# Layer 1, first pass: centring by 64x64 products, norm factors spread by 32-row products, and the second strip loaded earlier

## The chip, the core and the metric

The kernel runs on one core of a Trainium2 chip, in float32 throughout. The metric is device microseconds of one execution. Three executions of the kernel before took 8789.25 to 8792.47 us, with a median of 8791.17 us.

The core's engines are named as the profile names them: PE (TensorE, matrix products and transposes), PEld (its weight loads), DVE (VectorE), ACT (ScalarE), POOL (GpSimd) and SP (SyncE, which issues all the transfers here). Each engine works through its own queue in order; they wait for each other through semaphores.

## The reference, cut to what matters

The input is a 4 x 64 x 256 x 256 image. Layer 0 (a gated convolution) gives an image of the same shape. Layer 1, where the change lies, is this:

```python
def _layer_norm(x, g, b):
    mu = jnp.mean(x, axis=-1, keepdims=True)
    var = jnp.mean((x - mu) ** 2, axis=-1, keepdims=True)
    return (x - mu) * jax.lax.rsqrt(var + EPS) * g + b

def _s5_block(x, i, ...):
    fx = _layer_norm(x, ln1_g[i], ln1_b[i])
    h = _s5_scan(fx, ...)              # a linear recurrence, forward and backward
    x = jax.nn.gelu(h) + fx
    fx2 = _layer_norm(x, ln2_g[i], ln2_b[i])
    return fx2 @ ff_enc[i].T @ ff_dec[i].T + fx2

v = _gn(x)                             # group norm, 32 groups over 64 channels
y_h = _s5_block(v, row by row, 0)      # pixels in row order
y_v = _s5_block(v, column by column, 1)
x = x + concat([y_h, y_v], channels) @ fusion_w.T + fusion_b
```

The first layer norm runs over the 64 channels of each pixel, and both directions share it up to the gain `g` and the bias `b`: the centred and scaled value `z = (x - mu) * rsqrt(var + EPS)` is the same.

## The kernel before

Layer 0 comes first and writes its result into DRAM (`x1d[b]`, one per image `b`). Then, for each of the four images, `pass_a` and `pass_b` run one after the other. `pass_a` normalises the image, stores the normalised values `fv` (for the column direction) and `fh` (for the row direction) in DRAM for `pass_b`, and computes a summary of each group of 16 pixels along both directions. The scan at the start of `pass_b` turns the summaries into states, and the rest of `pass_b` computes the outputs. Only `pass_a`, and the few lines that load its strips, are changed.

`pass_a` works on 16 strips of 16 rows. A strip is loaded by four transfers of 256 KB into a tile `[128, 8, 256]`; the tile's two halves of 64 partitions hold 64 channels each, so that a column of the tile is two pixels. The ring of strip tiles has two buffers, which `pass_b` uses too. A software pipeline runs over 20 turns: in turn `n` strip `n` is centred, strip `n-1` gets its variances, strip `n-2` is scaled and stored, strip `n-3` gets its mirrored sums and differences, and strip `n-4` its summaries. The steps are functions, and a loop at the end of `pass_a` calls them in a fixed order. The wrappers `vec`, `act`, `gps` and `mm` keep the program's order on DVE, ACT, POOL and PE, so this order of calls is the order of every queue.

The steps before, with the tile names under which the profile lists them:

- `centre(s, i)`, four times in a strip: one 128x128 product over 512 columns (`pc`) subtracts the channel mean of both halves and applies the group norm; ACT reads the product twice, to write the centred values `xc` and the squares `sq`, 512 columns each.
- `sums(s)`: four products with 32 output rows each gather the squares into `pv`, and ACT copies it to `sums`.
- `rstd_of(s)`: four transposes (`pv`) bring the variances to two columns in 32; DVE adds the epsilon (`ve`), and POOL takes the power -1/2 (`rs`), in one instruction of 5.43 us.
- `widen(s)`: ACT puts the 32 factors of each partition back into PSUM, and DVE copies them 64-fold into `rw`, `[128, 32, 64]`.
- `affine(s, i)`, four times: four transposes of `rw` (`pr`) give the factors of 512 columns for all partitions; DVE multiplies them with `xc` and writes `z`, with the pixels of a row reordered.
- `scaled_in(s, i)`, four times: ACT writes `fv` and `fh` from `z`, with gain and bias.
- `mirrored(s, d)`: sums and differences of `fv` (DVE) or `fh` (POOL) with themselves mirrored (`sd`).
- `summary_columns(s, k)` (`pt`) and `summary_rows(s, k)` (`ps`): the products of the summaries, two groups each; ACT copies one half of each result to `m`.
- `place_columns(s)` and `place_rows(s)`: DVE adds and subtracts the halves into the state arrays `sf` and `sb`.
- `store(s)`: SP writes `fv` and `fh` to DRAM. The strip loads stand in the same SP queue.

In the order of calls, `affine`, `scaled_in` and `centre` alternate with the other steps in quarters of a strip. The helper lines of the profile are L1102 (`mm`), L1106 (transposes), L164 (ACT and POOL), L303 (DVE); a group is told by its tile names.

[...]

Of the kernel before, what the change touches and what calls it, by code (L numbers as in the profile page):

```python
# [11 lines left out]
AF = mybir.ActivationFunctionType  # L12
# [24 lines left out]
def _layout(parts):  # L37
    at, n = {}, 0
    for name, width in parts:
# [3 lines left out]


CONST_AT, CONST_N = _layout(
    [("ident", 128), ("swap", 128), ("nswap", 128), ("cen", 128), ("gm", 128), ("on2", 34), ("sgn", 1), ("qf", 64),
     ("qi2", 128), ("qj", 128), ("selt", 128)]
)

# [9 lines left out]
def _constants():  # L59

    out = np.zeros((P, CONST_N), np.float64)

    def put(name, a):
        o, w = CONST_AT[name]
        out[: a.shape[0], o : o + w] = a

    eye = np.eye(P)
    swap = np.roll(eye, C, axis=0)
    put("ident", eye)
    put("swap", swap)  # L70
    put("nswap", -swap)
    put("cen", eye - np.kron(np.eye(2), np.full((C, C), 1.0 / C)))
    pair = np.kron(np.eye(C // 2), np.ones((2, 2)))
    put("gm", np.kron(np.ones((2, 2)), pair) / 4.0)
    put("on2", np.kron(np.eye(2, 34, 2), np.full((C, 1), 1.0 / C)))
    put("sgn", np.concatenate([-np.ones((C, 1)), np.ones((C, 1))]))

    r, c = np.meshgrid(np.arange(8), np.arange(8), indexing="ij")  # L80
    q, sel = [], []
    for k1 in range(8):
        for k2 in range(5):
            own = k1 in (0, 4) and k2 in (0, 4)
            if k2 in (0, 4) and k1 > 4:
                continue
            w = np.zeros(40)
            w[k1 * 5 + k2] += 0.5
            w[((8 - k1) % 8 if k2 in (0, 4) else k1) * 5 + k2] += 0.5
            ang = 2 * np.pi * (k1 * r + k2 * c) / 8  # L90
            q.append(np.cos(ang).ravel() / 8 * (1 if own else math.sqrt(2)))
            sel.append(w)
            if not own:
                q.append(np.sin(ang).ravel() / 8 * math.sqrt(2))
                sel.append(w)
    q, sel = np.array(q), np.array(sel)
    assert q.shape == (64, 64) and np.allclose(q @ q.T, np.eye(64))
    put("qf", np.concatenate([q.T, q.T]))
    qi2 = np.zeros((2, 64, 2, 4, 2, 8))
    for pc in range(2):  # L100
        qi2[pc, :, :, :, pc] = q.reshape(64, 4, 2, 8).transpose(0, 2, 1, 3)
    put("qj", qi2.reshape(128, 2, 4, 8, 2).transpose(0, 1, 4, 2, 3).reshape(128, 128))
    for pc in range(2):
        qi2[pc, :, :, :, pc] = q.reshape(64, 2, 4, 8)
    put("qi2", qi2.reshape(128, 128))
    put("selt", np.concatenate([sel, sel]).T)
    return out.astype(np.float32)
# [3 lines left out]
def tile_kernel(ctx: ExitStack, tc: tile.TileContext, x, cst, w0, winp, wdwp, w1, out):  # L111
# [14 lines left out]
    def con(name):  # L126
        o, w = CONST_AT[name]
        return ct[:, o : o + w] if o < CONST_0 else tables[0][:, o - CONST_0 : o - CONST_0 + w]

    ident, swap, nswap = con("ident"), con("swap"), con("nswap")  # L130
    mhalf = new(cpool, [P, 32], "mhalf")
    nc.vector.memset(mhalf, -0.5)

# [941 lines left out]
        return t  # L1075


    norms = new(gpool, [P, nb, 2], "norms", 1)
    with tc.tile_pool(name="psn", bufs=2, space=PSUM) as pn:
        for b in range(nb):  # L1080
# [8 lines left out]
    def pass_a(b, x0):  # L1089
        with ExitStack() as es:  # L1090
            wp = es.enter_context(tc.tile_pool(name="wa", bufs=1))
            wk = es.enter_context(tc.tile_pool(name="wka", bufs=2))
            pp = es.enter_context(tc.tile_pool(name="psa", bufs=2, space=PSUM))
            wa = [new(wp, [P, NA[d], P], f"wa{d}") for d in range(2)]
            for d in range(2):
                nc.sync.dma_start(out=wa[d].rearrange("p a b -> p (a b)"), in_=wda[d])
# [8 lines left out]
                for k in range(4):  # L1105
                    tc.keep_in_program_order(nc.tensor.transpose(ps[:, k * P : (k + 1) * P], v(k), ident))  # L1106

            def centre(g, i):
                ps = new(pp, [P, 512], "pc")
                mm(ps, lhsT=cen, rhs=g["x"][:, 2 * i : 2 * i + 2, :].rearrange("p a b -> p (a b)"), start=True, stop=True)  # L1110
                xc, sq = new(wk, [P, 512], "xc", 9), new(wk, [P, 512], "sq", 5)
                act.activation(xc, ps, AF.Identity, bias=off)
                act.activation(sq, ps, AF.Square, bias=off)
                g["xc", i], g["sq", i] = xc, sq

            def sums(g):

                ps = new(pp, [P, 512], "pv", 1)
                for i in range(4):
                    mm(ps[32 * i : 32 * i + 32], lhsT=con("on2")[:, 2:34], rhs=g.pop(("sq", i)), start=True, stop=True)  # L1120
                g["sums"] = new(wk, [P, 512], "sums", 1)
                act.copy(g["sums"], ps)

            def rstd_of(g):

                ps, v = new(pp, [P, 512], "pv", 1), g.pop("sums")
                turn_blocks(ps, lambda k: v[:, k * P : (k + 1) * P])
                ve, r = new(wk, [P, 16, 2], "ve"), new(wk, [P, 32], "rs")
                vec.tensor_scalar(ve, ps.rearrange("p (n c) -> p n c", c=32)[:, :, 0:2], LN_EPS, None, ALU.add)
                gps.tensor_tensor(r, ve.rearrange("p n c -> p (n c)"), mhalf, ALU.pow)  # L1130
                g["rs"], g["by"] = r, ps

            def widen(g):

                g["r"], ps = new(wk, [P, 32, C], "rw"), g.pop("by")
                act.copy(ps[:, :32], g.pop("rs"))
                vec.tensor_copy(g["r"], ps[:, :32].unsqueeze(2).to_broadcast([P, 32, C]))

            def affine(g, i):

                if i == 0:
                    g["fv"], g["fh"] = new(wk, [P, 8, 256], "fv"), new(wk, [P, 16, 128], "fh")
                ps, z = new(pp, [P, 512], "pr"), new(wk, [P, 2, 16, 16], "z")
                turn_blocks(ps, lambda k: g["r"][:, 8 * k + 2 * i : 8 * k + 2 * i + 2].rearrange("p a c -> p (a c)"))
                vec.tensor_tensor(
                    z.rearrange("p r q g -> p r g q"), g.pop(("xc", i)).rearrange("p (r g q) -> p r g q", r=2, q=16),
                    ps.rearrange("p (r g q) -> p r g q", r=2, q=16), ALU.mult,
                )
                g["z", i] = z

            def scaled_in(g, i):
                z = g.pop(("z", i))
                act.activation(
                    g["fv"][:, 2 * i : 2 * i + 2].rearrange("p r (q g) -> p r q g", q=16), z, AF.Identity,
                    bias=par(1, "b1"), scale=par(1, "g1"),
                )
                act.activation(
                    g["fh"].rearrange("p q (r g) -> p q r g", r=8)[:, :, 2 * i : 2 * i + 2], z.rearrange("p r q g -> p q r g"),
                    AF.Identity, bias=par(0, "b1"), scale=par(0, "g1"),
                )  # L1160

            def mirrored(g, d):

# [50 lines left out]

            got = {0: {"x": x0}}

            def at(s, step, *args):
                if 0 <= s < NS1:  # L1220
                    step(got[s], *args)

            for n in range(NS1 + 4):
                if n + 1 < NS1:
                    got[n + 1] = {"x": load_strip(b, n + 1)}
                at(n, centre, 0)
                at(n - 2, affine, 0)
                at(n - 1, sums)
                at(n - 2, scaled_in, 0)
                at(n - 3, mirrored, 1)  # L1230
                at(n - 4, summary_columns, n - 4, 1)
                at(n - 1, rstd_of)
                at(n, centre, 1)
                at(n - 2, affine, 1)
                at(n - 2, scaled_in, 1)
                at(n - 4, place_columns, n - 4)
                at(n - 4, summary_rows, n - 4, 0)
                at(n, centre, 2)
                at(n - 2, affine, 2)
                at(n - 1, widen)  # L1240
                at(n - 2, scaled_in, 2)
                at(n - 4, summary_rows, n - 4, 1)
                at(n, centre, 3)
                at(n - 2, affine, 3)
                at(n - 4, place_rows, n - 4)
                at(n - 2, scaled_in, 3)
                at(n - 2, store, n - 2)
                at(n - 3, summary_columns, n - 3, 0)
                at(n - 3, mirrored, 0)

    def scan(tabs):
        with ExitStack() as es:
# [5 lines left out]
                nc.sync.dma_start(out=rot[d], in_=rotd[d])  # L1258

            fold = new(wp, [P, 3, C], "fold")  # L1260
            nc.vector.tensor_tensor(fold[:, 0], ident[:, 0:C], swap[:, 0:C], ALU.add)
            nc.vector.tensor_tensor(fold[:, 1], ident[:, 0:C], nswap[:, 0:C], ALU.add)
            nc.vector.tensor_tensor(fold[:, 2], ident[:, C:P], nswap[:, C:P], ALU.add)
            turns = [tabs[:, 4 * d : 4 * d + 4].rearrange("p (k a) c -> p k (a c)", k=2) for d in range(2)]
# [49 lines left out]
    def pass_b(b):  # L1314

        with ExitStack() as es:
# [201 lines left out]
            for n in range(len(order) + 3):  # L1518
                if n < len(order):
# [4 lines left out]
                    if d == 0 and s + 1 < NS1:  # L1524
                        accs[s + 1] = load_strip(b, s + 1)
                    elif d == 0 and b + 1 < nb:
                        accs[NS1] = load_strip(b + 1, 0)
                for i in range(4):
                    m, group = (n, 3) if i == 0 else (n + 1, i - 1)

# [16 lines left out]
                    late(1)  # L1547
        return accs.get(NS1)

    first = load_strip(0, 0)  # L1550
    for b in range(nb):
        pass_a(b, first)
        first = pass_b(b)
# [77 lines left out]
```

## Time and profile before

| Stretch of the profiled execution | us |
|---|---|
| its own time, from the first instruction to the last | 8795.4 |
| layer 0 (0 to 4041) | 4041 |
| first `pass_a`, from the first centring to the last summary | 260.0 |
| the other three, from the same point to the same point | 268.4, 269.2, 268.2 |
| all four | 1065.8 |
| one turn of `pass_a` in its steady part | 14.63 |

The profile recorded this one execution; its own time is its span, and there is no other record of it. The span is 4.2 us (0.05%) above the median of the three timed executions. PE was granted a clock of 0.988 on average.

The turn is taken from the starts of the first centring product of each strip. In the first image they stand at 4101.02, 4115.66, 4130.29, 4144.92 us and so on: from the sixth strip to the last one they are 14.63 us apart, in all four images. The first five turns of the first image take 6.55, 6.99, 14.53, 15.11 and 16.73 us. From the start of the last strip's first centring to the end of the last summary it takes 53.75 us.

A line of a list of groups reads: source line, engine, operation, output tile and input tiles, shapes, count, then busy time in total, the mean of one in ns, and the idle time of the engine before the group with what ended it. A line of a timeline reads: start, length, engine, line, operation, tiles, shapes and count of a run of equal instructions. Each float32 product appears as two matmuls.

### The profile page before, as it was taken

What the parts mean: (1) busy time and instruction counts of PE and PEld (TensorE: products, weight loads), DVE (VectorE), ACT (ScalarE), POOL (GpSimd) and SP (SyncE); (2) the same over time, 40 slices, a digit from 0 to 9 for tenths busy, and PEclk for the clock granted to TensorE, in tenths of its full rate; (3) what the DMA queues carried; (4) which work ended last, traced back from release to release, by engine and by line L of the source; (5) the groups of instructions that cost most, each with busy time, mean ns of one, the idle gap of its engine ahead of it and who ended that gap; (6) DMA issues with size and microseconds to landing.
All of it is one profiled execution on the core that took longest, in us unless ns stands there. A gap on an engine that the chain in (4) does not pass through costs nothing. (4 is left out here: it accounts for less than half of the span.)

```text
span 8795.4 us, 184922 instructions
## 1 busy us (share of the span) xinstructions
PE 8386.9 (95%) x79478; PEld 5721.3 (65%) x79478; DVE 7055.1 (80%) x8837; ACT 3411.4 (39%) x5158; POOL 2401.9 (27%) x1282
## 2 busy tenths in 40 slices
PE   3999999999999999998999989999989999899999
PEld 2666666666666666665566657566655666565666
DVE  6999999999999999996767657776757677576766
ACT  3444444444444444445522237222264222462222
POOL 3000000000000000003734446544456444474444
PEclk9999999999999999999999999999999999999999
DMA  7444344444444333334423336133263233452332
GB/s 174 106 102 103 98 103 101 104 102 98 103 104 101 87 88 84 84 80 142 151 68 82 91 90 214 59 80 89 73 183 116 80 82 80 123 196 53 82 89 65
DMA packets 655264, 904.19 MB, mean 103 GB/s; under 512 B 43120, under 2 KB 584816, under 8 KB 618864
## 3 DMA queue, kind: packets, MB, share of 16 engines
q1 hardware_dynamic: 654448, 892.37, 37.9%
q8 instruction: 627, 10.27, 0.5%
q14 instruction: 189, 1.55, 0.1%
HBM read 583.86 MB, written 275.05 MB: 98 GB/s over the span
## 5 line engine op out<-in xcount | busy, mean ns | idle before, releaser
L207 PE MATMUL m<-v,sw 64*128 64x256 f32 (+1 forms) x8192 | 1542.8, 393 | 1.5 <-DVE v L303 1.1
L207 PEld LDWEIGHTS m<-v,sw 64*128 64x128 f32 (+1 forms) x8192 | 1123.4, 188 | 504.0 <-issue 359.0
L303 DVE SCALAR_TENSOR_TENSOR acc<-xat,taps,acc 128x1024 f32<-128x1024 f32 x1024 | 1311.0, 1280 | 16.6 <-ACT acc L164 2.9
L1446 POOL TENSOR_TENSOR xr<-xr,fx 128x512 f32<-128x512 f32 x512 | 650.3, 1270 | 1862.3 <-ACT xr L1445 1367.7
L1351 PE MATMUL pst<-fx,wb 64*128 64x256 f32 (+1 forms) x4992 | 1016.1, 438 | 37.5 <-DVE stm L303 18.3
L694 POOL MEMSET at<- 64x256 f32 x4 | 1.2, 308 | 3526.2 <-DVE v L303 3526.2
L1351 PEld LDWEIGHTS pst<-fx,wb 64*128 64x128 f32 (+1 forms) x4992 | 508.8, 187 | 370.4 <-issue 244.1
L1476 POOL TENSOR_TENSOR rs<-ve,mhalf 128x32 f32<-128x32 f32 x128 | 695.3, 5432 | 99.5 <-DVE ve L303 99.5
L303 DVE SCALAR_TENSOR_TENSOR stm<-stm,step,pst 128x512 f32<-128x512 f32 x640 | 478.5, 748 | 232.9 <-PE pst L1351 219.4
L1447 ACT ACTIVATE sq<-xr 128x512 f32<-128x512 f32 x512 | 322.9, 631 | 873.7 <-POOL xr L1446 873.7
L207 PEld LDWEIGHTS m<-ct,hw 128*64 128x64 f32 x16384 | 509.8, 138 | 117.6 <-issue 117.6
L303 DVE SCALAR_TENSOR_TENSOR sto<-sto,step,pst 128x512 f32<-128x512 f32 x512 | 382.9, 748 | 242.4 <-PE pst L1351 231.1
L1351 PE MATMUL px<-wb,xr 128*128 128x128 f32 x4096 | 574.1, 284 | 0.0
L1351 PEld LDWEIGHTS px<-wb,xr 128*128 128x128 f32 x4096 | 524.2, 194 | 54.0 <-issue 41.8
L303 DVE TENSOR_TENSOR y<-px,rs 128x512 f32<-128x512 f32 x512 | 354.0, 691 | 230.6 <-PE px L1351 221.6
L1351 PE MATMUL ph<-sto,wb 128*64 128x128 f32 (+1 forms) x5120 | 528.1, 299 | 0.0
L207 PE MATMUL m<-ct,hw 128*64 128x64 f32 x16384 | 527.4, 223 | 0.0
L1351 PE MATMUL ph<-stm,wb 128*64 128x128 f32 (+1 forms) x5120 | 525.1, 299 | 0.0
L1351 PEld LDWEIGHTS ph<-stm,wb 128*64 128x64 f32 (+1 forms) x5120 | 409.3, 147 | 144.2 <-issue 127.9
L1351 PEld LDWEIGHTS ph<-sto,wb 128*64 128x64 f32 (+1 forms) x5120 | 405.3, 147 | 142.7 <-issue 129.6
L1445 ACT ACTIVATE xr<-ph 128x512 f32<-128x512 f32 x256 | 152.8, 597 | 825.9 <-PE ph L1351 825.9
L164 POOL TENSOR_TENSOR rs<-ve,mhalf 128x32 f32<-128x32 f32 x64 | 347.6, 5432 | 398.5 <-DVE ve L303 386.8
(317 smaller groups left out, 15636.0 us busy)
## 6 DMA issues: line engine op xcount, KB each, us to landing
strip<-x1d SPq DMA_DIRECT2D x512, 256.0 KB, 7.3
fx<-fxd SPq DMA_DIRECT2D x128, 1024.0 KB, 6.9
at<-in_x_dram SPq DMA_DIRECT2D x248, 320.0 KB, 4.6
sx<-in_x_dram SPq DMA_DIRECT2D x256, 256.0 KB, 4.0
pr<-in_x_dram SPq DMA_DIRECT2D x256, 256.0 KB, 4.1
er<-in_x_dram SPq DMA_DIRECT2D x256, 256.0 KB, 4.0
x1d<-x SPq DMA_DIRECT2D x256, 256.0 KB, 3.9
fxd<-fv SPq DMA_DIRECT2D x64, 1024.0 KB, 4.7
```

What stands on the lines that cost most here:

```text
L164: return lambda *args, **kw: tc.keep_in_program_order(getattr(self.engine, name)(*args, **kw))
L207: tc.keep_in_program_order(nc.tensor.matmul(*args, **kw))
L303: tc.keep_in_program_order(getattr(nc.vector, name)(*args, **kw))
L694: nc.gpsimd.memset(at[C:P, 4, 1 : S + 1], 0.0)
L1351: tc.keep_in_program_order(nc.tensor.matmul(*args, **kw))
L1445: nc.scalar.activation(xr, ps if d == 1 else xr, AF.Gelu_apprx_tanh)
L1446: nc.gpsimd.tensor_tensor(xr, xr, fx, ALU.add)
L1447: nc.scalar.activation(sq, xr, AF.Square)
L1476: nc.gpsimd.tensor_tensor(r, ve.rearrange("p n c -> p (n c)"), mhalf, ALU.pow)
```

## The change

The strips of `pass_a` are loaded so that a half of 64 partitions holds 8 neighbouring rows, as `[128, 2, 4, 256]`, again by four transfers of 256 KB. The steps that worked on quarters of a strip work on halves:

- `centre(s, k)`, twice in a strip: four 64x64 products over 512 columns into a tile of two banks, and ACT writes `xc` and `sq` with 1024 columns each.
- `rstd_of`: POOL writes its 32 factors into columns of a zeroed tile `wide`, two in each 32.
- `rows_back(s)` is new and takes the place of `widen`: four transposes of `wide` give the factors as rows, and DVE copies them out (`rows`). It stands at the head of the next turn, ahead of the centring.
- `affine(s, k)`, twice: two products of 32 rows by 128 columns over 512 columns, with a constant matrix `pick` of zeros and ones, spread the factors over the partitions. DVE multiplies 1024 columns into `z`.
- `scaled_in(s, k)`, twice: ACT writes 1024 columns of `fv` in one instruction, and `fh` in two of 512.

The centring and spreading products share one PSUM tag `two`, two buffers of two banks. The order of the loop is written anew; the second strip is loaded ahead of the matrices `wa` of `pass_a`. Elsewhere a constant `swap` is replaced by the negative of `nswap`.

```diff
+    def rows_at(s, k, hi):
+        row = s * R1 + 8 * hi + (k ^ hi)
+        return slice(hi * C, (hi + 1) * C), slice(row, row + 7, 2)
+
+    def load_sum(b, s):
+        t = new(ring, [P, 2, 4, S], "strip")
+        for k in range(2):
+            for hi in range(2):
+                half, rows = rows_at(s, k, hi)
+                nc.sync.dma_start(out=t[half, k], in_=x1d[b][:, rows, :])
+        return t
...
+            got = {0: {"x": x0}, 1: {"x": load_sum(b, 1)}}
             wa = [new(wp, [P, NA[d], P], f"wa{d}") for d in range(2)]
...
-            def centre(g, i):
-                ps = new(pp, [P, 512], "pc")
-                mm(ps, lhsT=cen, rhs=g["x"][:, 2 * i : 2 * i + 2, :].rearrange("p a b -> p (a b)"), start=True, stop=True)
-                xc, sq = new(wk, [P, 512], "xc", 9), new(wk, [P, 512], "sq", 5)
+            wide = new(wp, [P, 4, P], "wide")
+            nc.gpsimd.memset(wide, 0.0)
+
+            def centre(g, k):
+                ps = new(pp, [P, 2, 512], "two")
+                for h in range(2):
+                    for hi in range(2):
+                        p = slice(hi * C, (hi + 1) * C)
+                        mm(
+                            ps[h * C : (h + 1) * C, hi], lhsT=cen[p, p], rhs=g["x"][p, h, 2 * k : 2 * k + 2],
+                            start=True, stop=True,
+                        )
+                xc, sq = new(wk, [P, 2, 512], "xc", 6), new(wk, [P, 2, 512], "sq", 3)
                 act.activation(xc, ps, AF.Identity, bias=off)
                 act.activation(sq, ps, AF.Square, bias=off)
...
-                gps.tensor_tensor(r, ve.rearrange("p n c -> p (n c)"), mhalf, ALU.pow)
-                g["rs"], g["by"] = r, ps
-
-            def widen(g):
-                g["r"], ps = new(wk, [P, 32, C], "rw"), g.pop("by")
-                act.copy(ps[:, :32], g.pop("rs"))
-                vec.tensor_copy(g["r"], ps[:, :32].unsqueeze(2).to_broadcast([P, 32, C]))
+                gps.tensor_tensor(
+                    wide.rearrange("p k (i c) -> p (k i) c", c=32)[:, :, 0:2], ve,
+                    mhalf.rearrange("p (n c) -> p n c", c=2), ALU.pow,
+                )
+
+            def rows_back(g):
+                ps = new(pp, [P, 512], "pv", 1)
+                turn_blocks(ps, lambda k: wide[:, k])
+                g["rows"] = new(wk, [P, 512], "rows", 1)
+                vec.tensor_copy(g["rows"], ps)
...
-                ps, z = new(pp, [P, 512], "pr"), new(wk, [P, 2, 16, 16], "z")
-                turn_blocks(ps, lambda k: g["r"][:, 8 * k + 2 * i : 8 * k + 2 * i + 2].rearrange("p a c -> p (a c)"))
+                ps, z = new(pp, [P, 2, 512], "two"), new(wk, [P, 4, 16, 16], "z")
+                for hi in range(2):
+                    i = 2 * hi + k
+                    p = slice(32 * i, 32 * i + 32)
+                    mm(ps[:, hi], lhsT=con("pick")[p], rhs=g["rows"][p], start=True, stop=True)
...
             for n in range(NS1 + 4):
-                if n + 1 < NS1:
-                    got[n + 1] = {"x": load_strip(b, n + 1)}
+                if 0 < n and n + 1 < NS1:
+                    got[n + 1] = {"x": load_sum(b, n + 1)}
+                at(n - 2, rows_back)
                 at(n, centre, 0)
                 at(n - 2, affine, 0)
                 at(n - 1, sums)
                 at(n - 2, scaled_in, 0)
                 at(n - 3, mirrored, 1)
                 at(n - 4, summary_columns, n - 4, 1)
                 at(n - 1, rstd_of)
                 at(n, centre, 1)
+                at(n - 4, place_columns, n - 4)
+                at(n - 4, summary_rows, n - 4, 0)
                 at(n - 2, affine, 1)
                 at(n - 2, scaled_in, 1)
-                at(n - 4, place_columns, n - 4)
-                at(n - 4, summary_rows, n - 4, 0)
-                at(n, centre, 2)
-                at(n - 2, affine, 2)
-                at(n - 1, widen)
-                at(n - 2, scaled_in, 2)
                 at(n - 4, summary_rows, n - 4, 1)
-                at(n, centre, 3)
-                at(n - 2, affine, 3)
                 at(n - 4, place_rows, n - 4)
-                at(n - 2, scaled_in, 3)
                 at(n - 2, store, n - 2)
                 at(n - 3, summary_columns, n - 3, 0)
                 at(n - 3, mirrored, 0)
```

## The prediction

> **What bounds the kernel now.** I read the windows by stage first. They split the 8795.4 us of the profiled execution (4.2 us over the 8791.17 us median; differences are carried over unchanged) into layer 0, four first passes of 260 to 269 us and four second passes. Only the first passes change, so at most 1066 us are in play. The first line below is the whole first pass of image 0, the second a piece of its steady part (columns: window, length, then busy us and count of PE, PEld, DVE, ACT, POOL, then PE clock, DMA share, GB/s).
>
> ```profile
> 4041.00:4301.00 260.00, 242.21 (x1856) 168.68 (x1856) 170.41 (x225) 195.18 (x320) 164.77 (x48) 0.97 0.62 197
> 4090.00:4220.00 130.00, 129.52 (x1037) 92.81 (x1036) 91.11 (x125) 109.92 (x181) 90.89 (x27) 1.00 0.68 215
> ```
>
> In the steady part PE is busy for 129.5 of 130 us; ACT has work for 12.4 of each 14.63 us turn. Busy does not prove bound, so I read the timeline of one turn next:
>
> ```profile
> 4203.46 1.02 PE L1102 MATMUL pc<-strip,cenr 128*128 128x512 f32 x2
> 4204.31 0.60 PE L1106 MATMUL pr<-ct,rw 128*128 128x128 f32 x4
> 4204.85 1.07 PE L1102 MATMUL pv<-sq,ct 128*32 128x512 f32 x8
> 4205.84 2.00 PE L1102 MATMUL pt<-sd,wa 128*128 128x256 f32 x8
> 4207.67 0.60 PE L1106 MATMUL pv<-ct,sums 128*128 128x128 f32 x4
> 4208.11 1.02 PE L1102 MATMUL pc<-strip,cenr 128*128 128x512 f32 x2
> 4208.65 5.43 POOL L164 TENSOR_TENSOR rs<-ve,mhalf 128x32 f32<-128x32 f32 x1 [4.54 <-DVE ve L303]
> 4208.97 0.60 PE L1106 MATMUL pr<-ct,rw 128*128 128x128 f32 x4
> 4209.50 2.06 PE L1102 MATMUL ps<-sd,wa 64*128 64x128 f32 x32
> 4211.48 1.12 PE L1102 MATMUL pc<-strip,cenr 128*128 128x512 f32 x2
> ...
> 4215.67 0.35 ACT L164 COPY m<-ps 128x256 f32<-128x256 f32 x1
> ```
>
> No PE line carries an idle time, and start follows start: PE sets the turn. Prices are differences of starts: centring 0.86 (4208.11 to 4208.97), four transposes 0.44, square sums 0.86, `pt` 1.72, `ps` 1.78. A turn holds 4 x 0.86 + 4 x 0.44 + 0.86 + 0.44 + 2 x 1.72 + 2 x 1.78 = 13.5 us. The other 1.13 us lie at the six places where the shape of the PE array changes (`pr` to 128x32, back, `ps` and back): 0.19 us each.
>
> Last come groups by shape, for operations that the change makes longer or new:
>
> ```profile
> L164 ACT ACTIVATE en<-er,shift,rs 128x1024 f32<-128x1024 f32 x128 | 157.4, 1230 | 0.1
> L164 ACT ACTIVATE fv<-z,prm 128x512 f32<-128x512 f32 x256 | 208.5, 814 | 65.0 <-DVE z L303 64.5
> L303 DVE TENSOR_TENSOR z<-xc,pr 128x512 f32<-128x512 f32 x256 | 265.0, 1039 | 206.1 <-PE pr L1106 205.8 <-issue 0.3
> L303 DVE TENSOR_TENSOR sf<-pt,m 128x256 f32<-128x256 f32 x64 | 38.2, 596 | 14.5 <-ACT m L164 14.5
> L303 DVE COPY rw<-pv 128x2048 f32<-128x2048 f32 x64 | 146.7, 2292 | 54.7 <-ACT pv L164 54.7
> L303 DVE COPY m<-pv 128x64 f32<-128x64 f32 x128 | 27.4, 214 | 0.0
> L207 PE MATMUL two<-en,w0t 64*64 64x512 f32 x1024 | 139.5, 615 | 0.0
> ```
>
> **PE work, part by part.** The last line has 64x64 products of 512 columns: 1024 matmuls are busy for 139.5 us in 128 groups of four products, 1.09 us a group with overlap, so four run together in the time of one. Centring falls from 4 x 0.86 to 2 x 0.86. Spreading replaces 16 transposes (1.76) by two pairs of 32-row products. No row has 32 rows; the nearest is `ps`, pairs of 64 rows into two banks: 16 pairs of 128 columns in 1.78 us, 0.11 each, what one transpose of 128 columns takes alone. So 0.86 a pair (upper bound 1.72, one after the other). `rows_back` adds 0.44. Sum: 0.44 + 1.72 + 1.72 + 0.86 + 0.44 + 3.44 + 3.56 = 12.18 us. But the shape changes nine times in a turn, not six: 9 x 0.19 = 1.71, together 13.9 us. If PE stayed the bound, the turn would lose 0.74 us.
>
> [...] The `ps` row has pairs without loss, and I go by the row; nothing in this trace shows 32 rows.
>
> **What waits instead.** The new order closes a loop through four engines. Second spread (PE), `z` (DVE), `scaled_in` (ACT), then, behind it in ACT's queue, the copy of `ps` to `m`, which `place_rows` (DVE) needs; behind that in DVE's queue stands the copy of `rows`, and the next turn's first spread waits for that. Before, the copy of `ps` stood behind the third quarter's `scaled_in`, and the factors (`rw`) were copied ahead of the last quarter, so no product waited. Step by step:
>
> - First spread to second spread on PE, in order: 0.86 + 0.86 + 1.72 + 0.44 + 0.86 + 1.78 = 6.52, with five changes of shape 7.47.
> - Second spread to `z`: the two passes last 1.07 (as `pv`), handover 0.04 (`z` at 4213.09 starts so after `pr`): 1.11.
> - `z` of 1024 columns: 0.60 for 256 and 1.04 for 512 (both with scattered writes), so 0.88 more: 1.92. Bounds 1.57 (growing only as fast as the 128x2048 copy, 0.53 per 512) and 2.08 (two of today's).
> - `scaled_in`: 1.23 (`en`, 1024 columns) less 0.09 overlap, and twice 0.72 for `fh`: 2.58. Its first term lies between 0.94 (1.03, ACT's 1024 columns out of PSUM in layer 0, less 0.09) and 1.53 (today's two).
> - Copy to `m` 0.35, `place_rows` four starts of 0.195, 0.78; three handovers 0.12.
> - `rows`, 512 columns: between 0.21 for 64 and 2.29 for 2048 by length, 0.68; handover 0.05.
>
> Sum 15.06 us, against 14.63: plus 0.43 a turn, with PE idle for about 1.1 us ahead of the first spread. With all low values, and half of the changes of shape hidden in that idle time, the loop is 14.0; with the high ones 15.7 (a sixth change included). Queued behind the waiting spread on PE are `sums`, `pt`, the variance transposes and the second centring; ACT and POOL get their input later by as much.
>
> **Covered steps.** POOL's power keeps its 32 elements, but writes strided: after the first spread come `z` and two `sd` on DVE (3.0 + 2.3), `ve` 0.2, the power 5.43, so it ends at 11.1, and PE reaches `rows_back` at 12.1; it may grow by 0.9 us before it counts, and each 0.1 us beyond costs 0.1 us a turn. POOL's `sd` on `fh` (4.7 us) follows and ends 1 us into the next turn; its reader `ps` starts 5 us later. ACT drops to some 10 us a turn, DVE to 8.6 (`rw` goes): nobody waits for either in full. A strip's four loads keep their size and place behind the stores in SP's queue; their buffer comes free in mid-turn, and with 7.3 us to land they have half a turn to spare. The zeroing of `wide` (a memset of 64x256 is 0.35 us) lies beside the first centring. The `swap` edit exchanges equal DVE instructions.
>
> **First and last turns.** In the first ones the way round is variances, power, factors, spread, sums. It loses the copy back and `rw` (0.19 + 2.29) and gains `rows_back`, `rows` and a longer spread (0.60 + 0.68 + 0.42): minus 0.8 in two turns, minus 1.5 a pass (0 to minus 3). At the end before's turns get shorter as products fall away (the first spreads of the last three strips are 13.77 and 12.46 us apart). The loop keeps its 15.06 once and then loses one centring with its change of shape: 14.0. That is plus 1.3 and 1.5, and the last strip, scaled in halves rather than quarters, ends some 1.5 later: plus 4.3 (0 to 6).
>
> **Second strip.** In images 1 to 3 the centring of strip 1 waits until 5233.77, 7.3 us, for loads issued at 5226.47, after the second matrix transfer (5223.95). The loads still wait until the output leaves their buffer; what they gain is that transfer's place and 512 KB less beside them: minus 1.5 us each (0 to minus 3), three times. Image 0 waits for the group norm's factors, which the loads do not touch.
>
> **Sum.** A pass: -1.5 + 10 x 0.43 + 4.3 = +7.1; four passes +28; loads -4.5: +24 us, 8815 us. Own range 8795 (loop 14.7) to 8848 (loop 15.7).
>
> **Rivals.**
> 1. PE stays the bound and the kernel is faster. This is one mechanism: the loop is shorter than I sum it, because `z` and `fv` of 1024 columns cost less than twice 512. For it: the low bounds above. Against it: 256 and 512 columns fix the slope of `z`. At 13.9 us a turn a pass gains 7.4 + 1.5, four 36, with the loads 40: 8751 us. It decides from a loop below about 14.4 us.
> 2. The 32-row pairs run one after the other: 0.86 more in both spreads, both on the loop, 12 turns a pass: +20.6 a pass, 8897 us. For it: no row shows 32 rows; against it `ps`.
> 3. Nothing measurable: a loop near 14.6, with the ends cancelling: 8791 us.
>
> **How the numbers follow.** About 0.2%, 17.6 us, can be told from no change here. Forecast 0.62, of which 0.08 ends within 0.2%; rival 1 0.17; rival 2 with its partial forms 0.11; rival 3 0.10. Slower: 0.54 + 0.11 = 0.65; same 0.18; faster 0.17. For 8 in 10 the range takes half of rival 1 and a partial rival 2: 8762 to 8862.
>
> **What the profile after would show.** Right: firsts of centring 15.0 to 15.2 us apart, PE idle ahead of the first spread, released by `rows`, and `place_rows` on DVE just before it; `z` at 1.92, `fv` at 1.23 us; the spread pair some 1.07 us long. Wrong: PE without idle time at 13.9 us a turn (rival 1), or spread pairs of 1.9 us (rival 2). What would upset both is a longer power on POOL, with `rows_back` waiting for it.

## The result and the profile after

The changed kernel takes 8833.85 us (median; 8831.08 to 8839.12), the kernel before, run beside it, 8791.32. The ratio is 1.0048, with a 95% interval of 1.0033 to 1.0062: slower by 42.5 us, where 24 were forecast. The profiled execution of after has a span of 8831.5 us, 36.1 more than that of before (8795.4). The remaining 6.4 us are the places of the two profiled executions in the scatter of theirs: before's span lies 4.2 us above its median, after's 2.3 below. (A span is some 1.8 us shorter than the time of the same execution wherever both are recorded, so after's execution itself lay near its median and before's some 6 us above.) The parts below are parts of the 36.1.

First the windows of after, the whole first pass of image 0 and a piece of its steady part (columns: window, length, busy us and count of PE, PEld, DVE, ACT, POOL, then PE clock, DMA share, GB/s).

```profile
4041.00:4308.00 267.00, 235.11 (x1920) 142.48 (x1912) 141.33 (x195) 168.67 (x208) 163.95 (x49) 0.94 0.58 192
4090.00:4220.00 130.00, 121.16 (x1063) 77.20 (x1061) 74.01 (x102) 91.74 (x114) 88.48 (x27) 1.00 0.67 214
```

PE was busy for 129.5 of 130 us before and is now for 121.2, at full clock. It no longer sets the turn. Nor does any other engine: ACT's work falls to 91.7 us, DVE's to 74.0. Where all engines idle, a way round through several of them sets the time. The timeline of one steady turn shows it:

```profile
4204.71 0.35 ACT L164 COPY m<-ps 128x256 f32<-128x256 f32 x1
4205.09 0.29 DVE L303 TENSOR_TENSOR sf<-ps,m 128x128 f32<-128x128 f32 x1 [2.98 <-ACT m L164]
...
4205.89 0.68 DVE L303 COPY rows<-pv 128x512 f32<-128x512 f32 x1
4206.62 1.13 PE L1117 MATMUL two<-rows,ct 32*128 32x512 f32 x4 [1.11 <-DVE rows L303]
4207.68 1.07 PE L1117 MATMUL pv<-sq,ct 128*32 128x512 f32 x8
...
4214.04 1.13 PE L1117 MATMUL two<-rows,ct 32*128 32x512 f32 x4
4215.10 2.06 PE L1117 MATMUL ps<-sd,wa 64*128 64x128 f32 x32
4215.22 1.90 DVE L303 TENSOR_TENSOR z<-xc,two 128x1024 f32<-128x1024 f32 x1 [1.48 <-PE two L1117]
...
4217.15 1.24 ACT L164 ACTIVATE fv<-z,prm 128x1024 f32<-128x1024 f32 x1 [2.50 <-DVE z L303]
4218.30 1.51 ACT L164 ACTIVATE fh<-z,prm 128x512 f32<-128x512 f32 x2
```

Follow the starts. First spread 4206.62, second spread 4214.04 (7.42 later), `z` 4215.22 (1.18), `fv` 4217.15 (1.93). The turn repeats every 15.02 us, so the copy to `m` that follows starts at 4204.71 + 15.02 = 4219.73 (2.58 later). Then come `place_rows` (0.38), `rows` (0.80) and the next first spread (0.73). The sum is 15.02 us. PE stands still for 1.11 us in front of the first spread, for `rows`. The waits of nine turns show how regularly each link waits for the one ahead (columns: engine, line and releaser, then us in total, times, longest):

```profile
DVE sf L303 <- ACT m L164: 33.0, 18, 3.0
ACT fv L164 <- DVE z L303: 25.1, 18, 2.5
...
PE two L1117 <- DVE rows L303: 9.9, 9, 1.1
```

The groups by shape show the new durations (mean ns behind the comma): `z` 1.90 us, `fv` 1.24, `rows` 0.68. The power on POOL keeps its 5.44 although it now writes strided.

```profile
L164 POOL TENSOR_TENSOR wide<-ve,mhalf 128x32 f32<-128x32 f32 x64 | 347.9, 5436 | 396.8 <-DVE ve L303 396.8
...
L303 DVE TENSOR_TENSOR z<-xc,two 128x1024 f32<-128x1024 f32 x128 | 243.6, 1903 | 197.3 <-PE two L1117 187.6 <-issue 9.7
...
L164 ACT ACTIVATE fv<-z,prm 128x1024 f32<-128x1024 f32 x128 | 158.9, 1241 | 195.1 <-DVE z L303 195.1
...
L303 DVE COPY rows<-pv 128x512 f32<-128x512 f32 x64 | 43.6, 682 | 42.5 <-PE pv L1121 42.5
```

To place the 36.1 us I cut each pass at first spreads, the moments at which `affine` 0 of a strip starts on PE, and sum the four images:

| stretch | before, us | after, us | difference | predicted |
|---|---|---|---|---|
| first centring to first spread of strip 3 | 268.0 | 270.4 | +2.4 | -6.0 (first turns) - 4.5 (second strip) |
| first spread of strip 3 to that of strip 13 (ten steady turns) | 585.3 | 600.6 | +15.3 | +17.2 |
| first spread of strip 13 to the last `place_rows` | 211.6 | 227.8 | +16.2 | +17.2 |
| outside the first passes | | | +2.2 | 0 |

The steady turns and the end came as predicted, 31.5 against 34.4. The start should have given 10.5 back and took 2.4 instead. That is 12.9 us of a miss of 12.1 in the profiled executions. The 2.4 us are 3.0 gained up to the first spread of strip 0 (101.1 to 98.0 us) and 5.4 lost from there to that of strip 3 (167.0 to 172.4).

### The profile page after: what moved, and what is told of

It reads as the page before. It is cut to its first block, busy times and chain, and to the rows that moved or that the text cites. A ratio compares the mean times of both kernels' runs of the same rounds, so it can differ in the third digit from the quotient of the medians.

```text
span 8831.5 us, 184803 instructions
## 1 busy us (share of the span) xinstructions
PE 8382.8 (95%) x79734; PEld 5623.4 (64%) x79734; DVE 6934.0 (79%) x8709; ACT 3307.4 (37%) x4710; POOL 2396.2 (27%) x1286
## 5 line engine op out<-in xcount | busy, mean ns | idle before, releaser
L1508 POOL TENSOR_TENSOR rs<-ve,mhalf 128x32 f32<-128x32 f32 x128 | 695.4, 5433 | 99.3 <-DVE ve L303 99.3
L1383 PEld LDWEIGHTS px<-wb,xr 128*128 128x128 f32 x4096 | 524.6, 194 | 54.2 <-issue 41.8
L164 POOL TENSOR_TENSOR wide<-ve,mhalf 128x32 f32<-128x32 f32 x64 | 347.9, 5436 | 396.8 <-DVE ve L303 396.8
```

The lines of the kernel that those rows point to most:

```text
L164: return lambda *args, **kw: tc.keep_in_program_order(getattr(self.engine, name)(*args, **kw))
L1383: tc.keep_in_program_order(nc.tensor.matmul(*args, **kw))
L1508: nc.gpsimd.tensor_tensor(r, ve.rearrange("p n c -> p (n c)"), mhalf, ALU.pow)
```

## Experiments

The kernel before ran beside each and had medians of 8792.8 to 8795.9 us. Each result is given with its distance from the kernel before of the same group; on that scale the change itself is +42.5.

### Cutting the loop by the order of two calls

```
-                at(n - 2, scaled_in, 1)
                 at(n - 4, summary_rows, n - 4, 1)
+                at(n - 2, scaled_in, 1)
```

> Only the order of two calls changes: the second half of the row products, with its copy to m on ScalarE, is issued ahead of the second scaled_in, so that copy no longer stands behind scaled_in and place_rows no longer waits for z. The work on every engine is the same. Theory L (the loop spread - z - scaled_in - copy m - place_rows - rows - next spread sets the 15.02 us turn): the turn falls to the work of PE, 13.9 us by the prediction's sum (12.18 + nine changes of shape at 0.19); ten steady turns at -1.1 and about -3.5 in the last ones, times four: about -58 us, 8776 us (8765 to 8790). Theory P (PE itself got dearer: the small products and the changes of shape cost what the turn shows): turn 15.0 us, time unchanged at 8834 (8825 to 8842).

Measured: 8773.9 us, ratio to before 0.9976 (0.9965 to 0.9987), -18.9. The steady turn is 13.84 us in all images. In the timeline the copy to `m` now starts ahead of `fv`, and `rows` waits for PE alone:

```profile
4213.51 0.37 ACT L164 COPY m<-ps 128x256 f32<-128x256 f32 x1 [2.57 <-PE ps L1117]
4213.78 1.24 ACT L164 ACTIVATE fv<-z,prm 128x1024 f32<-128x1024 f32 x1
...
4215.81 0.69 DVE L303 COPY rows<-pv 128x512 f32<-128x512 f32 x1 [1.01 <-PE pv L1121]
...
4216.72 1.13 PE L1117 MATMUL two<-rows,ct 32*128 32x512 f32 x4
```

The first spread has no wait left. Not one operation was taken away or made shorter, and 61 us went. So the loop set the turn of 15.02 us, and the 13.84 are PE's own work, which the prediction summed to 13.9.

### Cutting the same loop on VectorE

```
-            for n in range(NS1 + 4):
+            for n in range(NS1 + 5):
...
                 at(n - 2, rows_back)
+                at(n - 5, place_rows, n - 5)
...
-                at(n - 4, place_rows, n - 4)
```

> The loop cut at another place, on VectorE: place_rows of a strip is issued one turn later, behind the next copy of rows; ScalarE's copy to m stays behind the second scaled_in and still comes late. PE's order is that of the kernel after. Theory L: rows no longer stands behind place_rows, the turn is PE's own, 13.84 us as with the row products ahead of scaled_in; with the last strip's place_rows a little later 8779 us (8768 to 8790). If the late copy to m itself held the turn through some other reader (the bank of ps that place_rows frees, or ScalarE's queue): 15.0 us a turn, 8834.

Measured: 8779.8 us, ratio 0.9982 (0.9973 to 0.9992), -15.4; the turn is 13.84 us. PE's order is untouched here, and the copy to `m` still comes late. It is `place_rows` ahead of `rows` on DVE that passed the delay on. From the first spread of the last strip to the end of its `place_rows` it takes 29.6 us, where the cut by the order of calls takes 27.0 to 28.6.

### The second spread ahead of the row products

```
                 at(n, centre, 1)
+                at(n - 2, affine, 1)
                 at(n - 4, place_columns, n - 4)
                 at(n - 4, summary_rows, n - 4, 0)
-                at(n - 2, affine, 1)
```

> The second spread and its z come directly behind the second centring, ahead of place_columns and of both halves of the row products; all else as after the change. Theory L: the loop is shorter by two halves of row products less one (1.78 + a change of shape), no longer the longest way round, and PE has eight changes of shape in a turn instead of nine: turn 13.7 us; per pass 10 x -1.3 and about -5 at both ends: -18, four passes -72, about 8762 us (8750 to 8778), below the kernel before. Theory P: only one change of shape goes, -0.19 x 12 x 4 = -9: 8825 us.

Measured: 8759.8 us, ratio 0.9962 (0.9947 to 0.9977), -32.9; the turn is 13.64 us. It differs from the 13.84 above by one change of the PE array's shape, eight instead of nine: 0.20 us, as the six in the turn before had given (0.19). With the prediction's 12.18 us of products, 13.64 is 0.18 for each of the eight. Steady windows of this kernel have PE busy throughout:

```profile
4100.00:4220.00 120.00, 120.00 (x1034) 75.61 (x1036) 75.78 (x106) 91.76 (x116) 88.00 (x28) 1.00 0.72 234
```

### The same extra work inside and outside the loop

```
                         AF.Identity, bias=par(0, "b1"), scale=par(0, "g1"),
                     )
+                if k == 1:   # k == 0 in the run outside the loop
+                    idle = new(wk, [P, 256], "idle", 1)
+                    for r in range(2):
+                        act.copy(idle, g["fv"][:, r])
```

> The same two copies, behind the first scaled_in instead: the same load on ScalarE, outside the loop. Theory L: turn stays 15.02, +0.7 a pass at the end, about 8837 (8830 to 8842). A theory in which the sum of ScalarE's work counts (longer strips of work on ACT make the turn): the same +33 as the copies behind the second scaled_in, 8867.

Measured outside: 8835.4 us, ratio 1.0048 (1.0033 to 1.0063), +42.7. The turn stays at 15.02 to 15.03 us although ACT has 0.7 us more to do in each. ACT's total is not on the path.

> After the second scaled_in of each strip ScalarE makes two more copies of 256 columns (0.3 us each from start to start, by the copy to m), whose result nobody reads. Theory L: they stand ahead of the copy to m, inside the loop: +0.6 us a turn, some 13 to 14 turns a pass, +8.4 a pass, about +33 us over the kernel after: 8867 (8858 to 8876). Theory P, and any in which ScalarE is not on the path (it has work for about 10 of 15 us): no change, 8834.

Measured inside: 8958.7 us, ratio 1.0190 (1.0174 to 1.0205), +165.9. That is 123 us over the kernel after, where 33 were expected. The direction is the loop's, the size is not. In image 0 the first two turns with the copies in them are 15.76 us, just 15.02 plus the 0.73 us by which `m` starts later. Then come turns of 17.4 and 19.05 us. The timeline of a long one, and its clock microsecond by microsecond:

```profile
4224.81 0.68 DVE L303 COPY rows<-pv 128x512 f32<-128x512 f32 x1
...
4225.54 1.59 PE L1117 MATMUL two<-rows,ct 32*128 32x512 f32 x4 [1.86 <-DVE rows L303]
...
4227.06 1.94 PE L1117 MATMUL pv<-sq,ct 128*32 128x512 f32 x8
...
4228.92 3.78 PE L1117 MATMUL pt<-sd,wa 128*128 128x256 f32 x8
```

```profile
4225.00:4226.00 1.00, 0.46 (x2) 0.30 (x4) 0.49 (x1) 0.99 (x1) 0.00 (x0) 1.00 1.07 451
4226.00:4227.00 1.00, 1.00 (x4) 0.00 (x0) 0.00 (x0) 0.00 (x0) 0.00 (x0) 0.54 0.97 401
...
4231.00:4232.00 1.00, 1.00 (x3) 0.81 (x3) 0.23 (x1) 1.00 (x2) 0.00 (x0) 0.50 0.00 0
4232.00:4233.00 1.00, 1.00 (x5) 0.73 (x4) 0.00 (x0) 0.45 (x2) 0.00 (x0) 0.55 0.00 0
4233.00:4234.00 1.00, 1.00 (x11) 0.27 (x9) 0.59 (x3) 0.12 (x1) 0.25 (x1) 1.00 0.00 0
```

PE waits 1.86 us for `rows`. Half a microsecond after the wait its granted clock drops from 1.00 to 0.50 and stays there for some 7 us; this is a turn of 19.05 us, and in those of 17.4 it stays there for 3.4. The square sums take 1.94 us instead of 1.07, `pt` 3.78 instead of 1.99. A wait on PE behind which the clock fell thus had two prices here, its length and the slow products behind it.

### A wait of medium length

One copy instead of the two, in the same place inside the loop.

> One copy of 256 columns instead of two behind the second scaled_in, so that PE waits about 1.5 us for rows in each turn: between the 1.11 us at which its clock stayed at 1.00 and the 1.85 us at which it fell to 0.50 in most turns. By the loop alone the turn is 15.02 + 0.37 = 15.39 us and the time 8834 + 13 x 0.37 x 4 = 8853 (8846 to 8860). If a wait of 1.5 us already costs the clock, turns of 17 us and more come back: over 8900.

Measured: 8890.0 us, ratio 1.0106 (1.0089 to 1.0123), +94.1. Neither of the two expectations holds: PE waits 1.41 us in each turn, and turns of 15.32 and of 16.96 us stand side by side in every image, in rows of several of the same kind. Under the same wait the clock is kept in some turns and lost in others.

The clock records of the traces show which. In those of the kernels before and after, 104 stretches at one granted clock last a whole multiple of 3.41 us each (only the last of either trace does not), and the low ones in the long turns of the runs with one copy and with two last 3.41 or 6.83. So the clock changed only at the marks of a grid of 3.41 us. Of the 44 waits of 1.4 us, 22 start 0.0 to 0.8 us after such a mark, and behind each of them the clock falls at the next mark, 1.2 to 2.0 us after the wait's end. The other 22 start 1.4 to 3.4 us after a mark, and the clock stays. With two copies, 40 of 44 waits cost the clock, and the four that do not all start 2.1 to 2.3 us after a mark. So in these runs the wait's place on the grid decided together with its length. The kernel after waits 1.11 us, and its steady turns keep a clock of 1.00 wherever the wait falls (it starts 0.1 to 3.4 us after a mark).

### Products that keep PE's clock up at the start of a pass

The failed part of the prediction lies in the first turns. The start of a pass at 15 us a window, first before (its first centring is at 5220.6), then after (first centring at 5227.3); the column behind POOL's is PE's clock:

```profile
5220.60:5236.00 15.40, 7.85 (x14) 2.46 (x18) 0.00 (x0) 5.03 (x9) 0.00 (x0) 0.72 1.00 235
5236.00:5251.00 15.00, 9.05 (x32) 2.59 (x24) 3.50 (x3) 7.28 (x14) 5.43 (x1) 0.85 0.49 101
5251.00:5266.00 15.00, 9.79 (x42) 4.97 (x43) 8.95 (x9) 12.66 (x20) 5.74 (x2) 0.83 0.57 167
```

```profile
5227.30:5243.00 15.70, 11.39 (x32) 2.12 (x32) 0.00 (x0) 5.96 (x6) 0.00 (x0) 0.50 0.98 247
5243.00:5258.00 15.00, 9.93 (x36) 2.75 (x36) 2.75 (x3) 5.12 (x7) 5.44 (x1) 0.50 0.37 84
5258.00:5273.00 15.00, 11.78 (x52) 3.83 (x52) 5.63 (x6) 11.43 (x13) 5.43 (x1) 0.62 0.58 188
```

PE's work on a strip has become shorter, and what is left of it stands between waits. In this image the clock does not rise for 42 us. Over the first 45 us of the four passes it is 0.65, 0.53, 0.61 and 0.50, against 0.83, 0.80, 0.77 and 0.76 before. The timeline of after shows the products at double length (centring 1.99 us, where the steady turn has 1.09) and the waits between them:

```profile
5235.27 5.86 PE L1117 MATMUL two<-strip,cenr 64*64 64x512 f32 x8 [4.30 <-DMA strip<-x1d]
5241.06 1.93 PE L1117 MATMUL pv<-sq,ct 128*32 128x512 f32 x8
...
5250.86 1.12 PE L1121 MATMUL pv<-ct,wide 128*128 128x128 f32 x4 [4.01 <-POOL wide L164]
5251.90 1.99 PE L1117 MATMUL two<-strip,cenr 64*64 64x512 f32 x8
...
5265.49 1.12 PE L1121 MATMUL pv<-ct,wide 128*128 128x128 f32 x4 [1.94 <-POOL wide L164]
```

The kernel after has one comparison of its own. From the first spread of strip 0 to that of strip 1 it takes 14.63 us in images 0, 1 and 3, all at a clock of 0.50, and 12.58 in image 2, where the clock rose in between (image 0, then image 2):

```profile
4058.29:4072.92 14.63, 11.93 (x44) 3.24 (x40) 4.62 (x4) 10.02 (x11) 5.43 (x1) 0.50 0.30 82
6453.29:6465.86 12.57, 8.03 (x44) 2.59 (x40) 4.67 (x4) 9.90 (x11) 5.43 (x1) 0.77 0.45 146
```

To test whether the clock makes these turns long, PE got work to do in its waits:

```
+            def spin(count):
+                ps = new(pp, [P, 512], "pt", 1)
+                for _ in range(count):
+                    mm(ps, lhsT=ident, rhs=ct[:, 0:512], start=True, stop=True)
...
+                if n in {1: 5, 2: 4, 3: 3}:
+                    spin({1: 5, 2: 4, 3: 3}[n])
                 at(n - 2, rows_back)
```

> The kernel after the change, with products that nobody reads (128x128 by 512 columns, into the bank of pt, which is not in use yet) on PE where it stands still in the first turns of a pass: five ahead of turn 1, four ahead of turn 2's rows_back, three ahead of turn 3's. Theory C (the first turns did not get shorter because PE, with less to do, runs them at a granted clock of 0.50: its 4.3 us between rows_back and the next variances count double): at full clock the first two turns of a strip's way round go from 14.6 to about 10.7 to 13 us and the first spread comes some 2.9 us earlier; about -8 a pass, -31 in all, 8803 us (8790 to 8815). Theory W (POOL's power and the order of the calls alone set these turns): nothing gained, the added products are at best hidden, 8834 (8832 to 8850).

Measured: 8825.1 us, ratio 1.0036 (1.0024 to 1.0049), +30.7, 12 us better than the kernel after. The window that had 0.50 has the full clock, and the same chain runs in it:

```profile
5243.00:5258.00 15.00, 11.27 (x55) 3.49 (x54) 2.42 (x3) 7.28 (x8) 5.44 (x1) 1.00 0.64 149
```

```profile
5255.22 1.13 PE L1117 MATMUL two<-rows,ct 32*128 32x512 f32 x4
...
5266.22 1.13 PE L1117 MATMUL two<-rows,ct 32*128 32x512 f32 x4
```

From the first spread of strip 0 to that of strip 1 it takes 11.00 us in all four images; in the kernel after it took 12.58 to 14.63. From the first spread of strip 0 to that of strip 3 the images together lose 13.1 us (172.4 to 159.3). So the clock did make these turns long. The time fell by 12 us and not by the 31 expected. Summed over the images the first spread itself came only 0.3 us earlier, where 2.9 a pass were expected: the five products ahead of turn 1 delay the centring of strip 1 where its load is there, in image 0 by 4.3 us. The turns behind it gave 13.1 us where some 20 were expected, and the end of the passes took 4.1 us more than in the kernel after.

### Strip 0's sums ahead of strip 1's centring

This run builds on the order with the early second spread.

```
+                if n == 1:
+                    at(0, sums)
+                    at(0, rstd_of)
                 at(n, centre, 0)
                 at(n - 2, affine, 0)
-                at(n - 1, sums)
+                if n > 1:
+                    at(n - 1, sums)
...
-                at(n - 1, rstd_of)
+                if n > 1:
+                    at(n - 1, rstd_of)
```

> The order with the early second spread, and in turn 1 alone the square sums and variances of strip 0 ahead of the first centring of strip 1, so that strip 0's power does not stand behind strip 1's load. Theory G (what the earlier load of strip 1 could give was lost because strip 0's factors wait in PE's queue behind that load): the first spread comes 2.8 us earlier in image 0 and about 6.4 in the other three, -22 us against the early spread's 8760: 8738 (8728 to 8752). Theory D (strip 1's own way through centring, sums and power sets the start in any case): 8760.

Measured: 8733.8 us, ratio to before 0.9930 (0.9915 to 0.9945), -60.7, and so 28 us less than the early spread alone. The first spread comes 1.0 us earlier in image 0 and 6.2 to 6.9 in the others. The timeline of image 1 has strip 0's sums and variances between the two strips' centrings:

```profile
5213.15 3.69 PE L1117 MATMUL two<-strip,cenr 64*64 64x512 f32 x16 [1.16 <-DVE strip L303]
5217.67 3.84 PE L1117 MATMUL pv<-sq,ct 128*32 128x512 f32 x8 [0.83 <-ACT sq L164]
5222.21 0.66 PE L1121 MATMUL pv<-ct,sums 128*128 128x128 f32 x4 [0.70 <-ACT sums L164]
5222.79 2.22 PE L1117 MATMUL two<-strip,cenr 64*64 64x512 f32 x6
```

Strip 0's power thus runs on POOL while strip 1 is still being loaded. In the kernel after, those sums stand in PE's queue behind the centring of strip 1, and so wait for strip 1's four loads, which they do not need.

Four unread products ahead of turn 3's `rows_back` were then added to this kernel, in the same form as above.

> The order of the last run (early second spread, strip 0's sums first) with four products that nobody reads on PE ahead of turn 3's rows_back, where PE stood still for 3.78 us and then ran 15 us at a clock of 0.50. Theory C (the clock lost in that wait costs the next turn): the clock stays at 1.00, that turn goes from 14.8 to about 11.6 us, -3 us a pass, -12 in all against 8734: 8722 (8714 to 8730). Theory W (the clock does not matter, power and loads set it): 8734, or up to 1 us a pass more.

Measured: 8737.5 us (8723.0 to 8746.4), ratio 0.9939 (0.9922 to 0.9955), -57.6. In the profiled execution the stretch to the first spread of strip 3 is 10.4 us shorter over the four images, of which 2.7 lie ahead of strip 0's first spread and so ahead of the products. From there to strip 1's first spread it takes 11.0 to 11.4 us instead of 12.0 to 14.6; the turn behind that, which was expected at 11.6, still takes 13.9 to 14.0. That execution is the fastest, with 8723.0. The median is no better than without the products, and the intervals overlap. Whether this pays stays open.

### The loads of the second strip alone

```
-            got = {0: {"x": x0}, 1: {"x": load_sum(b, 1)}}
+            got = {0: {"x": x0}}
...
-                if 0 < n and n + 1 < NS1:
+                if n + 1 < NS1:
                     got[n + 1] = {"x": load_sum(b, n + 1)}
```

> The kernel after the change with the second strip's loads behind the matrices again, as before the change. By the prediction's term the earlier loads are worth 1.5 us in three passes: 8838 (8834 to 8843). If PE's half clock and the wait for strip 0's power take all of it back: 8834, first spread of images 1 to 3 at the same distance from the first centring (26.4 to 26.8 us).

Measured: 8836.2 us, ratio 1.0050 (1.0037 to 1.0062), +41.8. In images 1 to 3 the first spread comes 28.7 to 29.5 us behind the first centring, 2.3 to 2.7 later than in the kernel after, and the four passes together are 5.9 us longer in the profile. In the time nothing of it can be told apart from the kernel after.

> The kernel before with one part of the change: the second strip's loads ahead of the matrices. By the prediction's term -1.5 in three passes: 8787 (8782 to 8791). If it is given back: 8791.

Measured: 8791.4 us, ratio 0.9997 (0.9988 to 1.0006), -3.0. The first passes together are 2.9 us shorter in the profile. In the passes of their profiles, one execution each, both runs agree in sign and size with a term of a few microseconds; neither is large enough for the time to show.

## Why the prediction was right in its sign and mechanism, and where its sum failed

**The loop (+17.2, measured +15.3): right.** The high bounds as they are listed add up to 15.8 us rather than 15.7; nothing rests on the difference. The predicted 15.06 us is 15.02, and its steps hold one by one: from spread to spread 7.42 us for 7.47, second spread to `z` 1.18 for 1.11, `z` with its handover 1.93 for 1.92 and 0.04, `scaled_in` 2.58 for 2.58, copy and `place_rows` with their handovers 1.18 for 1.13 and 0.08, `rows` with its handover 0.73 for 0.73. The 1.1 us for which PE was to idle ahead of the first spread are 1.11. Two different cuts of the loop bring 13.84 us; the same copies cost nothing outside it and more than their length inside.

**PE's work (13.9 us) and rival 1 (8751 us): the work was right, the rival was not.** With the loop cut, PE's own turn is 13.84 us, and nine changes of shape at 0.19 are confirmed by the run with eight. But the loop was longer, as forecast. Even with the cut the kernel stands at 8774 us and not at 8751: from the first centring to the first spread of strip 3 it takes 2.9 us more than before over the four images, where rival 1 had 10.5 less, and its ends take 6.7 us more, where rival 1 had nothing.

**The 32-row pairs (0.86 us), rival 2 (8897 us): right to go by the row of `ps`.** Start to start a pair takes 1.06 us, 0.86 plus a change of shape (0.19). No run shows a pair that loses only a part of the gain, the partial forms of rival 2 that the chances and the range count; these runs show no loss beyond the change of shape.

**Covered steps: right.** The power kept its 5.44 us, and `rows_back` does not wait for it in the steady turns. Rival 3, no measurable change, had the loop near 14.6; it is 15.02.

**The ends (+17.2, measured +16.2): right in sum, in part by luck.** The first longer turn came as predicted (5.3 us in the four images for 5.2). The second cost 9.4 us for 6.0, and the end of the last strip 1.5 for 6.0; these two misses cancel. The scatter between the images was not foreseen. The first spread of strip 14 waits 2.2 us in every image; in images 1 and 3 PE then runs `pt` at a clock of 0.50, in images 0 and 2 it does not. The timeline of after, image 0 and then image 3:

```profile
4266.76 1.13 PE L1117 MATMUL two<-rows,ct 32*128 32x512 f32 x4 [2.21 <-DVE rows L303]
...
4268.81 1.99 PE L1117 MATMUL pt<-sd,wa 128*128 128x256 f32 x8
...
7858.16 1.13 PE L1117 MATMUL two<-rows,ct 32*128 32x512 f32 x4 [2.22 <-DVE rows L303]
...
7860.29 3.56 PE L1117 MATMUL pt<-sd,wa 128*128 128x256 f32 x8
```

So the last two first spreads lie 14.0 us apart in images 0 and 2, and 15.6 in images 1 and 3. The grid of 3.41 us fits here too: the waits of images 0 and 2 start 2.1 and 2.3 us after a mark, those of images 1 and 3 0.5 and 2.7.

**The second strip (-4.5): right as far as it can be seen.** The undoing run and the run on the kernel before give 5.9 and 2.9 us in the passes of their profiles. The mechanism was only half of it. The first spread does come later when these loads do (2.3 to 2.7 us), but only because of the order on PE: once strip 0's sums no longer stood behind them, it came 6 us earlier in images 1 to 3.

**The first turns (-6.0): the step that failed.** The prediction listed what the way round variances, power, factors, spread, sums loses and gains, and priced every piece with durations of a steady turn at full clock. If the loads gave the 3 to 5.9 us that the two runs put on them, the first turns cost 5 to 8 us instead of giving 6. The runs put the granted clock in the place of that sum: 0.50 to 0.65 over the first 45 us of a pass, against 0.76 to 0.83 before, and turns of 14.63 us that become 11.00 when PE is kept busy. With the clock kept up, the stretch from the first spread of strip 0 to that of strip 3 takes 159.3 us over the images, 7.7 less than before. That the clock stayed down because less work on PE left shorter stretches between its waits is a guess of mine; no run tested it by itself. The windows of before already had the clock well under 1.00 in these turns; that column was the one to read.

**The rest.** 2.2 us outside the passes and the 6.4 us between profile and medians belong to no step.

## What to carry to other kernels

Sum the way round through all engines, in queue order, before believing that less work on the busiest engine shortens a loop; here the order of two calls was worth 61 us, more than the 42.5 that the change had cost. Price a wait on PE that can cost the clock (here 1.41 us did in 22 of 44 turns, 1.11 in no steady turn) at its length plus the products behind it at half clock (here for 3.41 or 6.83 us), and price the start of a stage at the clock that its windows show, not at that of the steady part. Where a stage begins with a load, put nothing behind the load in an engine's queue that does not need it: moving one strip's sums ahead of the next strip's centring gave 28 us, and with the early spread a kernel of 8734 us, 0.7% faster than before the change.

## What the runs showed of the hardware

- PE's clock fell after short waits. Once in a turn of some 15 us, a wait of 1.11 us kept it at 1.00, one of 1.41 us lost it in 22 of 44 turns (15.32 or 16.96 us), one of 1.85 us in 40 of 44 (15.76, or 17.4 to 19.05). The wait's place on the grid of 3.41 us told which turns escaped, as shown above. Just ahead of the wait stand four transposes and four 64x64 products in all three kernels; no run varied them.
- Once down in these turns, it stays at 0.50 for one or two steps of that grid although PE is busy throughout: for 3.41 us in each of the 22 turns of 16.96 us and in those of 17.4, for 6.83 in those of 19.05 (4226 to 4233 us above).
- A mirror sum `sd` that starts on DVE or POOL while the other engine's runs takes longer. In the kernel after, 115 of DVE's 128 overlap none of POOL's and last 1.18 to 1.22 us, and 115 of POOL's last 2.34 to 2.38. Where two meet, the one that starts second is longer by the overlap less 0.1 to 0.2 us (overlaps of 0.3 to 2.3 us), before the change as well. At 4293.41 DVE's starts 0.96 us into POOL's, lasts 2.48 us and ends 1.08 us after it; then POOL's next starts in DVE's second and lasts 3.40. The timeline (x2 is two instructions in a row):

```profile
4292.45 2.35 POOL L164 TENSOR_TENSOR sd<-fh 128x1024 f32<-128x1024 f32 x1 [3.38 <-ACT fh L164]
...
4293.41 3.61 DVE L303 TENSOR_TENSOR sd<-fv 128x1024 f32<-128x1024 f32 x2
...
4295.84 3.40 POOL L164 TENSOR_TENSOR sd<-fh 128x1024 f32<-128x1024 f32 x1 [1.03 <-PE ps L1117]
```
